# A state-space convolution block on one core: opening redone (x from two queues, output weights folded first, silus over two banks), pair six reordered, the next x's chunks from the third step

## The chip, the cores and the metric

The kernel runs on one core of a Trainium2 chip. Its time is the device time of one execution in microseconds; the time before is the median of three runs, 1819.84 us (1818.55 to 1820.01). The profile is of one further execution, 1821.96 us, of which the profiled span takes 1820.2 us.

## The reference

The input x is (4, 128, 96, 96). It is normalised in 32 groups of channels, read as four sequences of 9216 positions per batch element (rows forward and backward, columns forward and backward), put through the same block four times, and the four results are fused and added to x:

```python
t = _grouped1x1(x, in_proj_w, in_proj_b, G)
u, gate = (t[:, :HID], t[:, HID:])
u = jax.nn.silu(u)
u = lax.conv_general_dilated(u, dw_w, ..., feature_group_count=HID)     # 5 taps
s = _conv1x1(u, ssm_in_w)
a = DMIN + (DMAX - DMIN) * jax.nn.sigmoid(_conv1x1(u, ssm_delta_w, ssm_delta_b))
bb = jnp.tanh(_conv1x1(u, ssm_b_w, ssm_b_b))
cc = jnp.tanh(_conv1x1(u, ssm_c_w, ssm_c_b))
prefix = jnp.cumsum(jnp.log(a), axis=-1)
hst = jnp.exp(prefix) * jnp.cumsum(bb * s * jnp.exp(-prefix), axis=-1)
u = u + _conv1x1(cc * hst + ssm_d[None, :, None] * s, ssm_out_w)
u = _grouped1x1(u * jax.nn.sigmoid(gate), mix_w, mix_b, G)
return _conv1x1(u, out_proj_w, out_proj_b)
...
x = x + fuse(_scan1d of the four sequences of _gn(x))
```

B, DIM = 4, 128; HID, MH, G, K = 256, 32, 4, 5; everything is float32.

## The kernel before

**Tiles and stages.** A batch element is worked in two phases, columns ("V") and rows ("H"), and a phase treats its forward and its backward sequence together, as the units s = 0 and 1. A phase has NS = 6 steps of 16 lines, a step has R = 4 interleaved positions p, so a step is 8 units, worked as 4 pairs. There are 192 pairs in all. In the first half of a phase a step is "fresh": `front` computes the silus of its four position groups g out of x (`in_proj` on PE, `silu` on ACT). In the second half the backward sequence needs what the forward one had, so silus and gates are kept in DRAM (`keep_silu`, `kept`) and loaded again.

**A pair.** `pair(t)` writes the instructions of one pair by hand, for all engines in one order (a manual schedule: each engine and SP's queue run theirs in that order and wait for what they need). It contains:
- the convolution of pair t: half the channels by `taps` (five scaled additions; tap 0 is `first_tap`, on ACT at L628, one pair ahead, the other four are L630 on DVE), the other half by `conv` and `conv_less` on PE, copied to `u` by ACT (L609, L611);
- `front` of the position group four pairs ahead: in_proj (PE, L134 psum<-x_in,wn) and four silus (ACT, L470);
- `proj` (PE, L134 psum<-u,main), then tanh, copy and tanh on ACT (L667, L668, L673) and two operations on POOL (L675, L676); `scale_s` (ACT, L685) scales s of the pair before;
- `scan` on DVE (L702) once per half step, and `outputs` on POOL (L708, L709, L711) five pairs later;
- from pair LAG = 6 on, for the pair bi six pairs back: `gate` (PE, L491), `out_of` (PE, L497), `sigmoids` (ACT, L514), `gating` (DVE, L576 and L577), and one pair later `accumulate`: the output product (PE, L134 psum<-u,w_fin), a copy (ACT, L737) and an addition to acc (POOL, L754).

So pairs 0 to 5 are short, pairs 6 and 7 begin the gating, and from then on all parts run. PSUM has eight banks: 0 to 3 take gating's sums and 0 and 1 of them the taps too; 4 and 5 (PROJ) and 7, 6, 2, 3 (FRONT) change between conv, projection, front and gates. A product that writes a bank waits until ACT or DVE has read what was there.

**The opening.** ACT's queue loads `small`; SP's queue loads x of batch element 0 in ten transfers (24 chunks of 384 positions, 192 KB each) into `acc`, then fuse, main, the first x_in and the gates' x. A transfer is issued only when the one eight before it has landed. DVE takes bn_stats of each chunk (L298). `start()` then writes the rest: some filler products that read acc, `stats_finish` (mean, variance, sqrt, weights times the inverse deviation `wn`, bias `bn`), between its pieces `outer` (out_proj times fuse), then the bursts of in_proj for step 0 and sixteen silus of one bank each, `inner` (mix times that: `w_fin`), the first taps and conv, four keeps of silus, and the bias `b_fin`. x for step 1 is loaded when in_proj of step 0 has read the same tile. `proj` of pair 0 contains step 1's first front.

**The next x.** For batch elements 1 to 3 the statistics are taken during the V phase before: `chunks_of` names two chunks of the next x for the third and fourth pair of each of the six steps; `load_chunks` asks for them two pairs ahead (SP), and DVE takes their bn_stats in the pair (L387).

**What the steps of the prediction touch.** `load_x` (L294 to L298), `stats_finish` (L188 to L256), `chunks_of`, `after_front` and `keep_silu` (L450), `silu` (L470), `sigmoids`, `gates_and_out`, `gating`, `taps`, `proj`, `scale_s` (L685), `pair` and `start` (L992 to L1081).

Of the kernel before, what the change touches and what calls it, by code (L numbers as in the profile page):

```python
# [67 lines left out]
def conv_preact_kernel(  # L68
# [18 lines left out]
    accf = acc.rearrange("p h r m -> p (h r m)")  # L87
    x_in = [big.tile([P, R, N + 1], F32, name=f"x_in{s}") for s in range(2)]
# [65 lines left out]
    gmask = wp.tile([P, 4], F32, name="gmask")  # L154
    nc.gpsimd.memset(gmask, 1.0)
# [13 lines left out]
    stats, free = {}, [FRONT[1]]  # L169
# [10 lines left out]
    def stats_finish(b):  # L180
# [12 lines left out]
        nc.vector.tensor_copy(mean, pm[:, 0:1])  # L193
        dev = sp.tile([P, 1], F32, tag="dev", name=f"dev_{b}")
        nc.vector.tensor_sub(dev, mv[:, 0:1], mean)
        ex = sp.tile([P, 1], F32, tag="ex", name=f"ex_{b}")
        nc.vector.scalar_tensor_tensor(ex, dev, dev, mv[:, 1:2], ALU.mult, ALU.add)
        gm4 = sp.tile([P, 4], F32, tag="gm4", name=f"gm4_{b}")
        nc.vector.tensor_scalar_mul(gm4, gmask, mean)
# [9 lines left out]
        if b == b0:  # L209
# [4 lines left out]
            nc.vector.reciprocal(inv, std)  # L214
        else:
# [11 lines left out]
        yield  # L227
# [11 lines left out]
        product(pb[:, 0:4], wn, gm4)  # L239
        if b == b0:  # L240
            for g in range(4):
                for q in range(R):
                    mm(pb[:, 4 + g : 5 + g], q, wn[0:32, 32 * g : 32 * g + 32], mean[0:32, :], True, True)
            nc.vector.tensor_sub(bn, b_in, pb[:, 0:8])
        else:
# [10 lines left out]
        nc.vector.tensor_scalar_mul(bn[:, 2:4], bn[:, 2:4], 0.5)  # L256
# [8 lines left out]

    def load_front(step, s, r, q):
        if fresh(step):
            un = units[step * UB + s]
            nc.sync.dma_start(
                x_in[s][r, q, :], xs[un["b"], un["lay"], r, q, bass.ds(un["st"] * N, N + 1)]  # L270
            )
# [22 lines left out]
    def load_x(chunks):  # L294
        for c, n in chunks:
            nc.sync.dma_start(accf[:, bass.ds(c * SC, n * SC)], xr[b0, :, bass.ds(c * SC, n * SC)])  # L296
            for e in range(c, c + n):
                nc.vector.bn_stats(stats_of(b0)[:, e, :], accf[:, bass.ts(e, SC)])  # L298
# [5 lines left out]
    nc.gpsimd.memset(first_table, 1.0)  # L304
    nc.scalar.activation(first_table, first_table, AF.Sqrt)
    w_small = load(small, "small", nc.scalar)
    load_x([(0, 1), (1, 1), (2, 1), (3, 2), (5, 2), (7, 3), (10, 4), (14, 4), (18, 4), (22, 2)])
    w_out_fuse = load(fuse, "fuse")
    w_main = load(main, "main")
    for s in range(2):  # L310
        load_front(0, s, half(s), slice(0, R))
    for i in range(UB):
        load_gate(i)
# [50 lines left out]
    gates = [wk.tile([P, 2, 2, N], F32, tag=f"gate{e}", bufs=1, name=f"gate{e}") for e in range(2)]  # L364
# [7 lines left out]
    def chunks_of(t):  # L372

        un = units[2 * t]
        b, k = un["b"] + 1, t % R
        if un["order"] == "V" and b < B and k > 1:
            return [(b, un["st"] * R + 2 * (k - 2) + e) for e in range(2)]
        return []

    def load_chunks(t):  # L380
        for b, c in chunks_of(t):
            chunks[b, c] = wk.tile([P, SC], F32, tag="xs", bufs=4, name=f"xs_{b}_{c}")
# [52 lines left out]
    def after_front(step, g):  # L435
# [7 lines left out]
        if step > 1:  # L443
            keep_silu(1)
# [16 lines left out]
    def in_proj(step, g, s, j, bk):  # L461
        wn = stats[units[step * UB]["b"]][0]
        r = slice(64 * s + 32 * j, 64 * s + 32 * j + 32)
        for c in range(4):
            m, q = (c, g) if j else (g, R - 1 - c if s else c)
            mm(bank(bk), c, wn[r, s, 32 * m : 32 * m + 32], x_in[s][r, q, :], True, True)

    def silu(step, g, s, j, bk):
# [3 lines left out]
            bank(bk)[:, : N + 1],  # L472
            AF.Silu,
# [33 lines left out]
    def sigmoids(bi, to):  # L507
# [3 lines left out]
        for s in range(2):  # L511

            for j in (0, 1) if s == 0 or to[0] == GATE[True][0] else (1, 0):
# [30 lines left out]
    def gates_and_out(bi, with_front):  # L544

        to = GATE[with_front]
# [19 lines left out]
    def gating(bi, s):  # L566
# [8 lines left out]
        if bi not in seeded:  # L575
            nc.vector.tensor_add(pz, pz, v)  # L576
# [13 lines left out]
    def conv(i, banks):  # L590
# [3 lines left out]
        for s in range(2):  # L594
# [21 lines left out]
    def taps(i, ks, first=None):  # L616
# [5 lines left out]
        for k in ks:  # L622
# [6 lines left out]
            else:  # L629
                nc.vector.scalar_tensor_tensor(  # L630
                    us[i][:, :, 1, :] if k == K - 1 else part,
# [9 lines left out]

    def proj(i, banks, apart=False):
# [8 lines left out]
        turns = [(e, j) for j in ((1, 0) if i else (0, 1)) for e in range(2)]  # L651
        apart = apart or not i
        for e, j in sorted(turns) if apart and i else turns:
            if i == 0 and (e, j) == (0, 0):
                first = front_parts(R, (5, 4, 2, 3), half=True)
                next(first)
                next(first)
                first_tap(2)
                for _ in first:
                    pass  # L660
            for c, cols in enumerate(((qb, qb, qa, qa), (qs, qs, qc, qc))[e]):
                first, end = (j == 0, j == 1) if apart else (j == 1, j == 0)
                mm(bank(banks[e]), c, w_proj[:, j, cols], us[i][:, c % 2, j, :], first, end)
# [19 lines left out]
    def scale_s(i):  # L683
        s = tbs[i][0:64, :]
        nc.scalar.activation(s, s, AF.Copy, scale=d_sb[0:64, 0:1])  # L685
# [91 lines left out]
    def pair(t):  # L777
# [13 lines left out]
        if back:  # L791
# [13 lines left out]
        if t:  # L805
            new_u(i)
            taps(i, range(1, K))
            conv(i, banks)
        if t and not ahead:
            conv_less(i, banks)  # L810
        if not back and t:
# [71 lines left out]
        if not old and t > 0:  # L883
            scale_s(i - 2)
        if back:
# [102 lines left out]
    def start():  # L988
        w_of = wp.tile([P, 4, 2, P], F32, name="w_of")

        def filler(n):
            nc.tensor.matmul(  # L992
                bank(7)[:, :n], accf[:, bass.ds(10 * SC, P)], accf[:, bass.ds(10 * SC, n)],
# [3 lines left out]
        def outer(d, i, copy):  # L997
# [5 lines left out]
            copy(w_of[:, d].rearrange("p j c -> p (j c)"), bank(i)[:, : 2 * P])  # L1003

        def inner(ds, i):
# [6 lines left out]
            nc.vector.tensor_scalar_mul(to, bank(i), 0.5)  # L1012
# [160 lines left out]
```

## Time and profile before

| | |
|---|---|
| median of three runs | 1819.84 us (1818.55 to 1820.01) |
| the profiled execution | 1821.96 us, span 1820.2 us |
| busy: PE, ACT, DVE, POOL | 1792.3, 1562.5, 1454.6, 1428.2 us |
| DMA | 321 MB, mean 176 GB/s |
| last bn_stats of the first x ends | 18.82 us |
| first silu | 23.96 us |
| first projection | 35.22 us |
| tanh L667 of pairs 0, 5, 6, 7, 8 | 37.97, 68.50, 78.05, 88.71, 97.89 us |

A line of the timeline gives start and duration in us, engine, source line, operation, what is written and read with its shape, how many were merged, and in brackets the engine's idle time before it and what ended it. A line of the windows gives for each engine its busy time and instruction count, then the granted TensorE clock, the DMA engines' busy share and GB/s. A line of the chain gives start, duration and what the work that ended last waited for or did.

### The profile page before, as it was taken

The numbers are of one execution on the slowest core, as the hardware profiler recorded it, in microseconds if no ns is written. First come the engines' busy times: TensorE is split into PE (matmuls) and PEld (weight loads), VectorE is DVE, ScalarE is ACT, GpSimd is POOL, SyncE is SP. The second block draws the span as 40 slices with busy tenths as digits, with TensorE's granted clock in tenths as the row PEclk, the third lists the DMA queues.
The fourth block names the chain that finished last, engine by engine and source line by source line (L and its number), as shares of the span: only waits on it lengthen the run. The fifth ranks groups of instructions, "written<-read, shape, count | busy, mean of one in ns | idle before, by whom it ended". The sixth has DMA issues, their size and how long they took to land.

```text
span 1820.2 us, 56934 instructions
## 1 busy us (share of the span) xinstructions
PE 1792.3 (98%) x24074; PEld 645.5 (35%) x24074; DVE 1454.6 (80%) x1462; ACT 1562.5 (86%) x2748; POOL 1428.2 (78%) x1475
## 2 busy tenths in 40 slices
PE   6999999999999999999999999999999999999998
PEld 3333333333333333333333333333333333333333
DVE  6888878877888888877778888887877788778885
ACT  4888888988988888888888888888888888888974
POOL 3587878778778888788877888887877888887785
PEclk9999999999999999999999999999999999999999
DMA  8555463444975465334696456453477644635434
GB/s 246 175 190 179 149 203 99 162 142 154 313 242 181 158 196 171 119 135 137 224 296 227 141 179 210 119 171 110 161 237 223 227 148 129 197 102 177 149 125 155
DMA packets 148047, 321.17 MB, mean 176 GB/s; under 512 B 14160, under 2 KB 115920, under 8 KB 147792
## 3 DMA queue, kind: packets, MB, share of 16 engines
q1 hardware_dynamic: 147648, 317.48, 54.2%
q8 instruction: 190, 3.11, 0.7%
q14 instruction: 65, 0.53, 0.1%
q10 hardware_dynamic: 144, 0.04, 0.0%
HBM read 185.21 MB, written 132.25 MB: 174 GB/s over the span
## 4 chain that ended last, share of the span: by engine, by line
PE 94%; ACT 2%; DVE 2%; DMA 1%; issue 0%; SPq 0%; POOL 0%; DVEq 0%; ACTq 0%; POOLq 0%
PE psum L134 81%; PE psum L497 8%; PE psum L491 5%; DMA xs<-in_xr 1%; ACT psum L505 1%; ACT sil L470 1%; DVE psum L630 1%; DMA acc<-in_xr 0%; DVE bn L298 0%; ACT u L611 0%; DVE u L577 0%; DVE u L630 0%; ACT psum L628 0%; DVE t L702 0%; SPq L296 0%
## 5 line engine op out<-in xcount | busy, mean ns | idle before, releaser
L630 DVE SCALAR_TENSOR_TENSOR psum<-sil,small,psum 128x768 f32<-128x768 f32 x576 | 589.0, 1023 | 28.8 <-ACT psum L628 3.4
L134 PE MATMUL psum<-u,w_fin 128*32 128x384 f32 x6176 | 553.1, 488 | 0.2 <-ACT t L673 0.2
L577 DVE SCALAR_TENSOR_TENSOR u<-gate,psum 128x768 f32<-128x768 f32 x376 | 349.8, 952 | 249.0 <-ACT gate L514 107.2
L134 PE MATMUL psum<-u,main 128*32 128x384 f32 x6144 | 534.9, 489 | 1.6 <-DVE u L630 1.5
L754 POOL TENSOR_TENSOR acc<-ys,acc 128x384 f32<-128x384 f32 x374 | 410.7, 1120 | 32.1 <-ACT ys L735 10.8
L708 POOL TENSOR_TENSOR t<-t,t 64x384 f32<-64x384 f32 x191 | 232.3, 1216 | 153.8 <-DVE t L702 70.2
L134 PEld LDWEIGHTS psum<-u,w_fin 128*32 128x32 f32 x6176 | 188.9, 110 | 322.4 <-issue 216.6
L134 PEld LDWEIGHTS psum<-u,main 128*32 128x32 f32 x6144 | 181.9, 109 | 328.4 <-issue 200.7
L505 ACT COPY psum<-u 128x768 f32<-128x768 f32 x352 | 276.7, 799 | 23.1 <-DVE u L630 11.3
L134 PE MATMUL psum<-sil,band 128*32 128x384 f32 x3072 | 285.2, 488 | 0.0
L675 POOL TENSOR_SCALAR t<-tm 64x384 f32<-64x384 f32 x191 | 177.2, 928 | 123.2 <-ACT tm L667 104.2
L709 POOL TENSOR_TENSOR t<-t,t 64x384 f32<-64x384 f32 x191 | 246.8, 1292 | 15.0
L497 PE MATMUL psum<-t,main 32*128 32x384 f32 x1536 | 242.1, 514 | 3.3 <-ACT psum L505 2.6
L628 ACT ACTIVATE psum<-sil,small 128x768 f32<-128x768 f32 x191 | 173.2, 907 | 61.1 <-DVE u L577 52.8
L514 ACT ACTIVATE gate<-psum,bnorm 128x384 f32<-128x384 f32 x384 | 192.1, 582 | 30.1 <-PE psum L491 28.6
L676 POOL TENSOR_TENSOR t<-t,tm 64x384 f32<-64x384 f32 x192 | 195.1, 1016 | 15.3
L630 DVE SCALAR_TENSOR_TENSOR u<-sil,small,psum 128x768 f32<-128x768 f32 x192 | 194.9, 1015 | 7.8
L470 ACT ACTIVATE sil<-psum,bnorm 128x385 f32<-128x385 f32 x384 | 192.1, 585 | 3.7 <-PE psum L134 1.5
L134 PE MATMUL psum<-sil,less 64*32 64x384 f32 x3072 | 168.1, 495 | 0.0
L491 PE MATMUL psum<-x_in,wn 32*128 32x384 f32 x768 | 157.4, 526 | 3.0 <-DVE shift L249 1.4
L711 POOL COPY t<-t 64x384 f32<-64x384 f32 x188 | 141.2, 751 | 15.5 <-PE psum L134 3.6
L134 PEld LDWEIGHTS psum<-sil,band 128*32 128x32 f32 x3072 | 90.3, 109 | 169.6 <-issue 94.4
(102 smaller groups left out, 1484.3 us busy)
## 6 DMA issues: line engine op xcount, KB each, us to landing
sil<-sil SPq DMA_DIRECT2D x128, 770.0 KB, 6.8
kept<-gate SPq DMA_DIRECT2D x80, 768.0 KB, 3.7
gate<-kept SPq DMA_DIRECT2D x76, 768.0 KB, 5.1
x_in<-in_xs SPq DMA_DIRECT2D x192, 96.2 KB, 2.5
out<-acc SPq DMA_DIRECT2D x48, 384.0 KB, 8.0
acc<-in_xr SPq DMA_DIRECT2D x39, 384.0 KB, 6.9
xs<-in_xr SPq DMA_DIRECT2D x72, 192.0 KB, 5.5
x_in<-in_xs SPq DMA_DIRECT2D x46, 192.5 KB, 3.5
```

Of the source, the lines that this page charges most:

```text
L134: nc.tensor.matmul(o[r, : rhs.shape[-1]], lhsT, rhs, start=start, stop=stop, skip_group_check=True)
L470: nc.scalar.activation(sils[step][:, s, j, g, :], bank(bk)[:, : N + 1], AF.Silu, bias=bn[:, 1:2] if j else bn[:, 4 + g : 5 + g],)
L491: nc.tensor.matmul(bank(to)[:, :N], stats[un["b"]][0][r, s, :], x_in[s][r, q, off : off + N], start=True, stop=True)
L497: nc.tensor.matmul(bank(SSM + 2 * s + j)[:, :N], w_so[r, bass.ts(j, P)], z[r, :], start=bi not in seeded, stop=True, skip_group_check=True)
L505: nc.scalar.copy(psum[:, SSM + 2 * s : SSM + 2 * s + 2, :N], us[bi][:, s])
L514: nc.scalar.activation(gv[:, s, j, :], bank(to[2 * s + j])[:, :N], AF.Tanh, bias=bn[:, 2 + j : 3 + j], scale=0.5,)
L577: nc.vector.scalar_tensor_tensor(v, g, 1.0, pz, ALU.add, ALU.mult)
L630: nc.vector.scalar_tensor_tensor(us[i][:, :, 1, :] if k == K - 1 else part, src, w_tap[:, k : k + 1], part, ALU.mult, ALU.add,)
L676: nc.gpsimd.tensor_mul(ta[0:64, p, :], tb[0:64, :], tm[0:64, :])
L708: engine.tensor_mul(ta[0:64, p, :], tb[64:P, :], ta[64:P, p, :])
L709: engine.tensor_add(tb[0:64, :], ta[0:64, p, :], tb[0:64, :])
L754: adder.tensor_add(part, y, part)
```

## The change

It does ten things. (1) x of batch element 0 is asked for from two queues, SP's and ACT's, seven transfers each with small and fuse among them; fuse comes before chunk 10. (2) main is asked for only after bn_stats of chunk 16, through a one-column DVE copy that it has to follow; the gates' x and both steps' x come after it on SP. (3) Step 0 has its own x tile, `x_first`, so step 1's x is loaded in the opening too; the second gate buffer lies in `x_first` later. (4) `outer` and `inner` come before `stats_finish`, with all their copies on ACT; `w_of` uses a slot of the tag "u". (5) In `stats_finish` for the first batch element the bias products use the unscaled weights and a `gm4` that holds the inverse deviation, and the order of a few small operations changes. (6) The sixteen silus of step 0 become eight over two banks each, in an order that starts with a second-half group; five of step 0's taps become two ahead of the others, and DVE does pair 1's first tap. (7) The four keeps of step 0 are issued one per front of step 1, and `b_fin` is computed at the end of pair 2, its addition on DVE. (8) `scale_s` runs on POOL for the first five pairs. (9) In pair 6 the front's silus are split around conv, `out_of` comes before the gates, and both seed additions before both gatings. (10) The next x's chunks are three per pair in the third to sixth steps instead of two in all six.

The diff, cut to its core:

```diff
-    def load_x(chunks):
+    def ask_x(queue, *chunks):
         for c, n in chunks:
-            nc.sync.dma_start(accf[:, bass.ds(c * SC, n * SC)], xr[b0, :, bass.ds(c * SC, n * SC)])
-            for e in range(c, c + n):
-                nc.vector.bn_stats(stats_of(b0)[:, e, :], accf[:, bass.ts(e, SC)])
+            queue.dma_start(accf[:, bass.ds(c * SC, n * SC)], xr[b0, :, bass.ds(c * SC, n * SC)])
+    def stats_x(chunks):
+        for c in chunks:
+            nc.vector.bn_stats(stats_of(b0)[:, c, :], accf[:, bass.ts(c, SC)])
...
+    ask_x(nc.sync, (0, 1), (2, 1), (4, 1), (6, 2))
+    ask_x(nc.scalar, (1, 1), (3, 1))
+    w_small = load(small, "small", nc.scalar)
+    ask_x(nc.scalar, (5, 1), (8, 2))
+    w_out_fuse = load(fuse, "fuse")
+    ask_x(nc.sync, (10, 3), (16, 4))
+    ask_x(nc.scalar, (13, 3), (20, 4))
     nc.scalar.activation(first_table, first_table, AF.Sqrt)
-    w_small = load(small, "small", nc.scalar)
-    load_x([(0, 1), (1, 1), (2, 1), (3, 2), (5, 2), (7, 3), (10, 4), (14, 4), (18, 4), (22, 2)])
-    w_out_fuse = load(fuse, "fuse")
-    w_main = load(main, "main")
+    stats_x(range(17))
+    w_main = wp.tile(list(main.shape), F32, tag="main", name="main")
+    nc.vector.tensor_copy(w_main[:, 0:1], stats_of(b0)[:, 16, 0:1])
+    nc.sync.dma_start(w_main, main)
+    stats_x(range(17, NSC))
     for s in range(2):
         load_front(0, s, half(s), slice(0, R))
+    for s in range(2):
+        load_front(1, s, half(s), slice(0, R))
...
-        if un["order"] == "V" and b < B and k > 1:
-            return [(b, un["st"] * R + 2 * (k - 2) + e) for e in range(2)]
+        if un["order"] == "V" and b < B and k > 1 and un["st"] > 1:
+            return [(b, 3 * (2 * un["st"] + k - 6) + e) for e in range(3)]
...
-        if step > 1:
+        if step > 0:
             keep_silu(1)
...
+    def both_silus(step, g, j, b0):
+        bn = stats[units[step * UB]["b"]][1]
+        nc.scalar.activation(
+            sils[step][:, :, j, g, :],
+            psum[:, b0 : b0 + 2, : N + 1],
+            AF.Silu,
+            bias=bn[:, 1:2] if j else bn[:, 4 + g : 5 + g],
+        )
...
+        to = GATE[with_front] if bi else (4, 5, 7, 6)
+        if bi == 0:
+            for s in range(2):
+                for j in range(2):
+                    out_of(bi, s, j)
+            for s in range(2):
+                for j in range(2):
+                    gate(bi, s, j, to[2 * s + j])
+            sigmoids(bi, to)
+            return
...
-        if bi not in seeded:
+        if bi == 0 and s == 0:
+            for e in range(2):
+                pe = psum[:, SSM + 2 * e : SSM + 2 * e + 2, :N]
+                nc.vector.tensor_add(pe, pe, us[bi][:, e])
+        elif bi and bi not in seeded:
             nc.vector.tensor_add(pz, pz, v)
...
+        if i < 2 * LAG - 2:
+            nc.gpsimd.tensor_scalar_mul(s, s, d_sb[0:64, 0:1])
+            return
...
-        if back:
+        if bi == 0:
+            turned = front_parts(t + R, (2, 3, 7, 6), half=True)
+            next(turned)
+            next(turned)
+        elif back:
             front(t + R, FRONT)
...
+        if bi == 0:
+            for _ in turned:
+                pass
...
+        if t == 2:
+            at_two[0]()
...
+        def b_final():
+            pf = bank(3)[:, 0:1]
+            terms = [(w_of[:, 0, j, :], b_mix[:, j : j + 1]) for j in range(2)]
+            terms.append((w_fuse[:, 0, :], b_out))
+            for c in range(4):
+                for n, (lhsT, rhs) in enumerate(terms):
+                    mm(pf, c, lhsT[:, 32 * c : 32 * c + 32], rhs, n == 0, n == 2)
+            nc.vector.tensor_add(b_fin, pf, b_fuse)
+        at_two.append(b_final)
+        for d in range(4):
+            outer(d, (0, 1, 4, 5)[d])
+        inner((0, 1), 2)
+        inner((2, 3), 3)
...
+        filler(512)
+        filler(256)
+        next(pieces)
+        next(pieces)
+        filler(256)
+        next(pieces)
+        filler(256)
+        next(pieces)
...
+        order = [(1, 0)] + [(0, g) for g in range(R)] + [(1, g) for g in range(1, R)]
+        spots = (D, A, C, D, A, C, A, C)
...
+        for n in range(3):
+            burst(*order[n], spots[n])
+        silus(*order[0], D)
+        burst(*order[3], D)
+        taps(0, (0,), nc.vector)
+        taps(0, (R,), last=3)
+        silus(*order[1], A)
+        burst(*order[4], A)
...
+        silus(*order[7], C)
+        conv_less(0, head_banks(0))
+        taps(0, (3,), last=3)
+        taps(2, (0,), nc.vector)
...
+        front(R, (5, 4, 2, 3))
```

Here D, A and C are the bank pairs (6, 7), (2, 3) and (4, 5).

## The prediction

> **What bounds the kernel now.** First the page: is any engine always busy, and where is it not?
>
> ```profile
> span 1820.2 us, 56934 instructions
> PE 1792.3 (98%) x24074; PEld 645.5 (35%) x24074; DVE 1454.6 (80%) x1462; ACT 1562.5 (86%) x2748; POOL 1428.2 (78%) x1475
> PE   6999999999999999999999999999999999999998
> ```
>
> PE is full in all slices but the first and the last. Listing every start of tanh L667 (one per pair) shows the same: from pair 8 (97.89 us) on the pairs follow each other by 9.11 to 9.33 us, with shorter and longer ones only where a phase or its half changes. So an opening that is redone can only move the moment at which this beat sets in; I forecast that shift. Second, the chain of waits up to 90 us:
>
> ```profile
> 3.62 8.53 DMA acc<-in_xr
> 12.17 6.66 DVE bn L298 x14
> 18.86 0.82 DVE mv L188
> ...
> 36.15 12.76 DMA xs<-in_xr
> 48.94 1.06 DVE bn L387 x2
> ...
> 53.07 1.02 DVE u L630
> 54.23 4.97 PE psum L134 x64
> ```
>
> Until 18.82 the kernel waits for x and its statistics; at 48.94 a chunk of the *next* x ends a wait that pushes taps and projection. Third, the stretches by window: is x held by issue or by transfer?
>
> ```profile
> 2.00:4.00 2.00, 0.00 (x0) 0.00 (x0) 0.37 (x1) 0.74 (x2) 1.81 (x9) 1.00 1.02 254
> 4.00:6.00 2.00, 0.00 (x0) 0.00 (x0) 0.90 (x3) 0.00 (x0) 1.93 (x7) 1.00 0.78 210
> 8.00:12.00 4.00, 0.00 (x0) 0.00 (x0) 3.34 (x7) 0.00 (x0) 2.93 (x8) 1.00 1.03 421
> ```
>
> The last two columns are the DMA engines' share and GB/s: the engines have work from 2 us on, move 210 to 254 GB/s up to 6 us and 421 after. So it is the transfer, not its issue, from 6 us on. Fourth, the timeline, for prices:
>
> ```profile
> 24.90 5.32 ACT L470 ACTIVATE sil<-psum,bnorm 128x385 f32<-128x385 f32 x11 [0.36 <-PE psum L134]
> 48.00 1.99 ACT L470 ACTIVATE sil<-psum,bnorm 128x385 f32<-128x385 f32 x4
> 48.94 1.06 DVE L387 BATCH_NORM_STATS2 bn<-xs 128x6 f32<-128x384 f32 x2 [2.38 <-DMA xs<-in_xr]
> 55.35 1.42 SPq L450 DMA_DIRECT2D sil<-sil  x1
> 79.16 0.88 PE L134 MATMUL psum<-x_in,wn 32*32 32x385 f32 x16 [0.57 <-DVE u L577]
> 186.19 1.82 DVE L577 SCALAR_TENSOR_TENSOR u<-gate,psum 128x768 f32<-128x768 f32 x2 [1.08 <-PE psum L497]
> ```
>
> The first row is eleven silus back to back (0.484 each), the second the four silus behind projection 2, then the late chunk, one keep of silus (770 KB, its issue held), PE waiting for pair 6's gating, and DVE's idle time in a steady pair with chunks.
>
> **The change, in five stretches.** Marks of before: last bn_stats ends 18.82; first silu 23.96; projections of pairs 0 to 7 (PE, psum<-u,main) start at 35.22, 41.48, 47.32, 54.23, 60.08, 65.83, 75.00, 86.53.
>
> *1. x (to the last bn_stats).* ACT's issues (0.41 each) cost nothing: ACT idles until 20.73. Each queue now gets seven transfers before the last bn_stats, and fuse (512 KB) moves ahead of chunks 10 to 23. Landings before: chunks 0 to 4 by 7.87, 0 to 23 by 16.92, so 19 chunks (3648 KB) in 9.05 us, 403 KB/us. After: 3648+512 KB at that rate is 10.3 us. If the ramp is as before, x is in at 7.87+10.3 = 18.2; if both queues reach the plateau from the first bytes (2.2), at 2.2+(960+4160)/403 = 14.9. No row shows two large queues at once, so I take the middle, 16.6. The queues are paired size for size, so the last two transfers (16-19 and 20-23) should land together, and eight bn_stats of 0.475 plus the 0.2 us marker copy for main still follow: end at 20.6 (18.9 to 22.2). Before, DVE had only 1.9 us left after the last landing. **+1.8** (+0.1 to +3.4). [...] Main is held until bn_stats 16, and x_first, step 1's x and all gate loads queue behind it on SP: main (384 KB, 1 to 1.85 us) and two halves of x_first (1.75 each, 20.35 to 22.10 to 23.86 before) arrive some 2.5 to 3.4 us after the last bn_stats, before they are needed; if later, all is late by that.
>
> *2. Last bn_stats to first silu.* Before 5.14, as the second half of x_in landed only at 23.86. After: the 3.74 us to wn lose the mean copy (0.19) and the wait behind outer (some 0.2), gain gm4 (0.24): 3.6; then in_proj 0.33 issue and 0.5 latency: 4.45. Outer and inner ran after the last bn_stats; now they follow fuse (in by about 10) with their copies on ACT, and with the fillers are over between 17 and 19, so PE idles 3 to 5 us before the mean product (1.0 before). Two readings show what that may do: the filler's matmuls are 0.85 us apart up to 16.5 and 0.43 after, and in the tail a half-idle stretch is followed by half the granted clock (the column after POOL):
>
> ```profile
> 1794.00:1798.00 4.00, 1.98 (x12) 0.89 (x10) 2.57 (x4) 1.98 (x3) 3.74 (x4) 1.00 0.02 4
> 1798.00:1804.60 6.60, 6.60 (x37) 1.89 (x36) 1.91 (x2) 2.66 (x5) 5.35 (x5) 0.51 0.19 74
> ```
>
> I charge 0.4 for a first burst at half speed (0 to 1.5): 4.85. **-0.3.**
>
> *3. First silu to projection 0.* Before 11.26: sixteen silus of 0.484 with inner's 2 us and b_final between. After: eight silus over two banks, 0.80 each (L611, the same width out of PSUM, 0.799), end 6.85 after the first, one slot lost to PE; the last tap adds 1.02 and handoffs end at 8.05; conv_less and u's copy (0.80) end at 8.15 beside it. Projection 0 at 8.2. POOL's w_of adds (3.3 us, once main has come) and edges, and DVE's first two taps, hide under the silus; if they did not, the adds would delay the edges by about their own length. The front of step 1 (four silus, 2.0) fits between u's copy and projection 0's tanh. **-3.06** (0.5 either way).
>
> *4. Pairs 0 to 5, projection to projection.* Before 6.26+5.84+6.91+5.85+5.75 = 30.61. Undisturbed, PE's order (projection 2.28, conv 1.75, less 0.81, in_proj 1.03) makes 5.87. The chunk stall goes: pair 3 alone had 6.91. scale_s on POOL (0.93, POOL is idle 3.7 to 4.9 us per pair) frees 0.62 of ACT that PE's beat hides. But two waits come. b_final now stands behind projection 2 on PE and needs bank 3, which the last silu of that front frees 2.7 us after the projection's start (48.00+1.99 against 47.32 above); conv 3 waits behind it, and its tensor_add on DVE ends at 3.6, with pair 3's four taps (4.15, and 0.1 to PE) queued behind: projection 3 at 7.85, **+2.0** on 5.87 (at least +1.0, since without bank 3's wait it follows the projection itself). And the keeps of step 0, four in a row at 32 to 36 us before, now go out one per front, the last in pair 3, while pair 4's first silu reuses that tile. The row at 55.35 is the same place in SP's queue, behind the four x loads of pair 3: it landed at 61.98, and the silus stood at 60.76. Some 1.2 us of wait on ACT; behind it stand that pair's tanh and the banks of conv 5, so 0.83 on PE (0 to 2). Sum 5.87+5.87+7.87+5.87+6.70 = 32.18. **+1.6.** (-0.2 to +2.8)
>
> *5. Pairs 6 and 7.* out_of comes before the gates, so DVE's seed adds start some 2 us earlier; gating ends at 11.05 after projection 5 instead of 13.27, and the 0.57 of idle at 79.16 goes, as does pair 7's bn_stats. PE's next conv_less moves from 15.57 to 14.2 and all behind it with it: **-1.25** (-1.4 to -0.5). Later pairs: a third bn_stats (0.5) meets at least 1.08 us of DVE idle (186.19): 0. If that cover were gone, 24 pairs by up to 0.5.
>
> Sum: 1.8-0.3-3.06+1.6-1.25 = -1.2 on the profiled execution (1821.96, span 1820.2), which stands 2.1 above the median; on the median 1819.84 that is **1818.6**. What stage 3 gains, stages 1 and 4 give back.
>
> **Rivals.** *A, faster:* both queues run at the plateau at once, bn_stats end at 18.9, PE stays at full clock (-0.4), the keep lands in time (-0.8), b_final costs only 1.0. -1.2-1.7-0.4-0.8-1.0 = -5.1, 1814.7. For it: the slow stretch up to 6 us is that of the single chunks, with the shortest rows (1536 bytes), which a second queue could overlap; against: the engines' share is 1.02 from 2 to 4 us already.
>
> *B, slower:* TensorE stays at half clock through projection 0 and pair 1. Stage 3 would gain conv 0.65, less 0.65, front 0.65, projection 2.3 = 4.25 behind the last silu, pair 1 again 4.9: -1.6+9.1 = +7.5, 1827.3. It decides from about 1 us after projection 0's end. For it: the tail's row of 0.51 after a half-idle stretch; against: burst and conv at half speed keep PE 80% busy. [...]
>
> *C, the second queue does nothing:* ramp as before, end at 22.2, +0.4 in all, 1820.2.
>
> **How the numbers follow.** 0.2% (3.6 us) is about what a measurement here can tell from no change. My forecast 0.32 and C 0.20 lie within it: same 0.52. A and its neighbours below 1816.2: faster 0.33. B and a later x: slower 0.15. The low bound is A's time less 1.0, half of what it would bring if chunks 16-19 landed one transfer (1.9) ahead of 20-23; the high one is the slow ends of stages 1, 2 and 4 together (1.6+1.1+1.2 above the forecast, 1822.5) and 1 us of B.
>
> **What would show it.** Right: last bn_stats near 20.6, with eight after one landing; projection 0 near 33.6; a DVE wait for b_final's matmuls after pair 2 and an ACT wait on a keep in pair 4; pair 5 where it was; pair 7 1.25 earlier; then 9.11. Wrong: x in by 15.5, projection 0 before 32 or after 36, granted clock 0.5 beyond 34, or pairs after 8 off their beat.

## The result, and the profile after

The changed kernel takes 1829.73 us (median of 6 runs, 1828.0 to 1830.32) beside 1819.92 for the kernel before (6 runs): ratio 1.005 [1.004, 1.0059], slower by half a per cent. The forecast was 1818.6, with 1823.5 as the high end. The profiled execution took 1830.32 (span 1828.6), 8.4 more than that of before, and the tanh of pair 8 (now L713) starts at 106.43 instead of 97.89, 8.54 later; the beat behind it is 9.11 as before. So the loss lies wholly in the first 100 us, and the marks split it:

| stretch | before | after | change | forecast |
|---|---|---|---|---|
| 1. to the end of the last bn_stats | 18.82 | 23.50 | +4.69 | +1.8 |
| 2. to the first silu | 5.14 | 6.21 | +1.06 | -0.3 |
| 3. to projection 0 | 11.26 | 13.09 | +1.83 | -3.06 |
| 4. projection 0 to 5 | 30.61 | 33.20 | +2.59 | +1.6 |
| 5. projection 5 to 7 | 20.70 | 19.06 | -1.64 | -1.25 |

Executions of one kernel differ, and the longest have the lowest mean granted clock (before: 31 executions taken together, from 1818.57 to 1827.74, clock 0.999 to 0.994); each ratio below is therefore against the kernel before on the same chip at the same time, over all executions (it is not the ratio of the two medians), and mechanisms are read from the marks. A mark comes from one trace of each kernel.

First the page of the changed kernel. The first slice, of 45.7 us, is the only one that differs much from before: PE 5 tenths (6 before), granted clock 0.7.

```profile
span 1828.6 us, 56961 instructions
PE   5999999999999999999999999999999999999998
PEclk7999999999999999999999999999999999999999
```

Second, its chain of waits (start, length, what):

```profile
6.36 13.28 DMA acc<-in_xr
19.66 1.94 DVE bn L311 x4
21.60 0.05 DVE main L328
21.65 1.86 DVE bn L311 x4
...
57.97 0.16 DVE b_fin L1083
...
63.21 5.89 DMA sil<-sil
...
71.66 0.13 ACT sil L499
```

x comes to 19.63 (16.92 before), and eight bn_stats stand behind the last landing, as forecast. The marker copy for main (L328) runs after twenty bn_stats and not after seventeen: the program was not run in its written order. SP's issues say the same, with x_first (two halves of step 0's x) 12.9 us ahead of main:

```profile
8.79 1.31 SPq L280 DMA_DIRECT2D x_first<-in_xs  x2
21.68 0.34 SPq L329 DMA_DIRECT2D main<-in_main  x1
```

Further down the chain stand the two waits that were forecast, b_final's add and a keep ahead of pair 4's silus. Third, the windows (the column after POOL is the granted clock, then the DMA engines' share and GB/s):

```profile
20.00:24.00 4.00, 0.00 (x0) 0.00 (x0) 3.96 (x10) 0.00 (x0) 0.00 (x0) 0.62 0.35 86
24.00:28.00 4.00, 3.52 (x72) 2.17 (x76) 1.78 (x9) 1.48 (x2) 0.38 (x1) 0.50 1.07 243
28.00:32.00 4.00, 4.00 (x79) 1.86 (x78) 1.41 (x4) 2.50 (x5) 0.18 (x2) 0.50 0.74 177
36.00:40.00 4.00, 4.00 (x40) 0.63 (x32) 1.69 (x2) 1.62 (x2) 0.00 (x0) 0.50 0.01 4
```

TensorE has nothing at all from 20 to 24, and from then on half the clock: the trace's clock records have 0.5 from 20.96 to 41.44. In the last two rows PE is full (4.00 of 4) while the number of matmuls in a window falls to 40, and ACT, which should bound the silus, is busy 1.62 of 4. Fourth, rows of the timeline (start, busy, what, and the idle time before it with its releaser):

```profile
24.48 0.29 PE L135 MATMUL psum<-mv,gmean 128*32 128x1 f32 x8 [7.17 <-DVE mv L190]
57.97 0.16 DVE L1083 TENSOR_TENSOR b_fin<-psum,small 128x1 f32<-128x1 f32 x1 [4.18 <-PE psum L135]
62.37 2.79 PE L135 MATMUL psum<-u,main 128*32 128x384 f32 x32 [1.44 <-DVE u L681]
71.66 2.00 ACT L499 ACTIVATE sil<-psum,bnorm 128x385 f32<-128x385 f32 x4 [2.57 <-PE psum L135]
72.77 1.50 PE L135 MATMUL psum<-sil,band 128*32 128x384 f32 x16 [1.76 <-ACT sil L499]
```

The 7.17 us of idle time ahead of the mean product had been forecast as 3 to 5. DVE's 4.18 ahead of b_fin and PE's 1.44 ahead of projection 3 are b_final's wait; ACT's 2.57 and PE's 1.76 are the keep's. ACT's row names PE because the profile puts a wait for several things down to one; the chain names the keep, whose landing it puts at 69.10, and leaves 2.48 us behind it unexplained. The two runs below that change only the order and the queues of the opening's loads have the same wait (2.55 and 2.37 on ACT) and a full record of the landing: the silus start at 69.72 and 68.12, 0.15 behind the landing of that keep (69.57 and 67.97). So the keep most likely landed at about 71.5 here.

### The profile page after: what moved, and what is told of

Read it like the earlier page. It is cut to its first block, busy times and chain, and to the rows that moved or that the text cites. A ratio compares the mean times of both kernels' runs of the same rounds, so it can differ in the third digit from the quotient of the medians.

```text
span 1828.6 us, 56961 instructions
## 1 busy us (share of the span) xinstructions
PE 1794.7 (98%) x24088; PEld 646.7 (35%) x24088; DVE 1451.7 (79%) x1453; ACT 1558.1 (85%) x2736; POOL 1438.0 (79%) x1489
## 4 chain that ended last, share of the span: by engine, by line
PE 95%; ACT 2%; DMA 1%; DVE 1%; issue 0%; ACTq 0%; DVEq 0%; SPq 0%
PE psum L135 82%; PE psum L535 8%; PE psum L529 5%; DMA acc<-in_xr 1%; ACT psum L543 1%; ACT sil L499 1%; DVE psum L681 0%; DMA sil<-sil 0%; ACT u L662 0%; DMA small<-in_small 0%; DVE bn L311 0%; ACT psum L679 0%; PE psum L1054 0%; DVE u L681 0%; DVE u L628 0%
## 5 line engine op out<-in xcount | busy, mean ns | idle before, releaser
L628 DVE SCALAR_TENSOR_TENSOR u<-x_first,psum 128x768 f32<-128x768 f32 x188 | 174.9, 953 | 127.3 <-ACT x_first L552 61.0
L628 DVE SCALAR_TENSOR_TENSOR u<-gate,psum 128x768 f32<-128x768 f32 x188 | 174.8, 953 | 115.5 <-ACT u L660 57.1
L499 ACT ACTIVATE sil<-psum,bnorm 128x385 f32<-128x385 f32 x368 | 183.9, 583 | 4.7 <-PE psum L135 2.6
```

The source lines that it names most:

```text
L499: nc.scalar.activation(sils[step][:, s, j, g, :], bank(bk)[:, : N + 1], AF.Silu, bias=bn[:, 1:2] if j else bn[:, 4 + g : 5 + g],)
L628: nc.vector.scalar_tensor_tensor(v, g, 1.0, pz, ALU.add, ALU.mult)
```

## The experiments

**Is it the gap on TensorE, through the clock?** The changed kernel with six more fillers of 512 columns:

```
-        filler(512)
-        filler(256)
+        for n in (512,) * 7 + (256,):
+            filler(n)
```

> Six more filler matmuls of 512 columns on TensorE ahead of the mean product, where the changed kernel has 7.17 us of idle time. Theory (idle TensorE brought the half clock, and the half clock made the opening long): granted clock 1.0 from about 14 us on; last bn_stats unchanged at 23.5; first silu about 5.4 after it (6.20 with the half clock); projection 0 starts 8.5 after the first silu (13.09), so about 37.4 instead of 42.80; all later marks 5.4 earlier; median about 1824.4. Rival 1 (the eight silus and their handoffs set the length, the clock little): clock 1.0, but projection 0 still 11 or more after the first silu, gain under 2.5, 1827.3 or more. Rival 2 (the clock falls for another reason than idle time): 0.5 from about 21 us again, 1829.7.

Measured: 1824.57 (ratio to before 1.0024 [1.0014, 1.0033]). Windows:

```profile
20.00:24.00 4.00, 2.81 (x8) 1.14 (x6) 3.97 (x10) 0.00 (x0) 0.00 (x0) 1.00 0.44 111
24.00:28.00 4.00, 2.99 (x100) 1.92 (x101) 1.95 (x10) 1.69 (x3) 0.39 (x1) 1.00 1.08 240
28.00:32.00 4.00, 3.67 (x90) 1.02 (x63) 2.10 (x3) 3.61 (x5) 0.56 (x6) 1.00 0.74 175
```

The last bn_stats ends where it did (23.51), the clock stays at 1.0, the first silu comes 4.89 behind it (4.85 forecast) and projection 0 9.38 behind that, at 37.77. Compared with the changed kernel's 6.21+13.09 the half clock costs 5.03 of stretches 2 and 3. In four other traces with the half clock (the runs below on order, queue, b_final and keeps) the two stretches take 19.2 to 20.3, against 14.27 here. Where stretch 3 still misses the forecast (9.38 against 8.2), ACT waits for PE's products: idle 0.43 and 0.73 ahead of the last two silus and 0.69 ahead of u's copy. The ten executions range from 1822.05 (clock 0.997) to 1829.01 (0.993): some still meet the half clock, and the traced one, at 0.998, does not show where.

**Does idle time do the same to the kernel before?** Its six fillers taken out:

```
-        for n in (512, 512, 512):
-            filler(n)
-        for n in (512, 512):
-            filler(n)
-        filler(128)
```

> The kernel before, without its six filler matmuls: TensorE has nothing to do until the mean product at 19.8. Theory (idle TensorE alone brings the half clock, whatever the opening's order): granted clock 0.5 when the chain begins and until about 35 to 41, last bn_stats unchanged at 18.8, first silu 0.5 to 1.2 later, projection 0 3 to 5 us later than 35.22; tanh of pair 8 at 101 to 103; median 1823 to 1825. Rival (the half clock in the changed kernel comes from its small in_proj matmuls and the fillers matter little): clock 1.0 within 4 us of the first products, projection 0 under 1.5 later, median under 1821.5.

Measured: 1826.49, ratio 1.0024 [1.0009, 1.0038]; last bn_stats at 18.26, first silu 7.75 behind it (5.14), projection 0 at 40.53 instead of 35.22. The trace has no clock record before 34.60, where 1.0 begins; the durations tell:

```profile
24.44 6.99 PE L134 MATMUL psum<-x_in,wn 32*32 32x385 f32 x96
31.36 3.58 PE L1007 MATMUL psum<-w_of,fuse 128*128 128x128 f32 x16
```

The same rows in the kernel before:

```profile
23.07 4.58 PE L134 MATMUL psum<-x_in,wn 32*32 32x385 f32 x96
27.58 2.05 PE L1007 MATMUL psum<-w_of,fuse 128*128 128x128 f32 x16
```

TensorE was slow through all its bursts, and full speed was there at the end of the 3.41 us that inner's 128-row matmuls fill to 95%. `outer`, which has 128 rows too, had filled 78% of an earlier such stretch (20.95 to 24.37) and not brought it back. With TensorE idle ahead of the chain (for 7.17 us in the changed kernel, until 19.25 here) either opening was slow, which speaks for the theory; in this trace the loss was larger than expected. But the gap is not enough by itself: of the ten executions six take 1825.9 to 1828.3 and four 1820.2 to 1823.0, near the kernel before.

**Why did it stay down for 20 us of busy work?** Three wide fillers in the middle of the changed kernel's bursts, at half clock:

```
             burst(*order[n], spots[n])
+        for _ in range(3):
+            filler(512, 0)
         silus(*order[0], D)
```

> The changed kernel, with three filler matmuls of 128 rows by 512 columns behind the first three bursts of in_proj, that is, in the middle of the stretch at half clock. [...] Rival (once lowered the clock stays down for a set time, three periods of 6.83 us): back at 41.4 as before, projection 0 some 4 to 5 us later; median over 1833.

```profile
28.00:32.00 4.00, 4.00 (x35) 1.58 (x19) 0.06 (x1) 2.49 (x3) 0.37 (x4) 0.50 0.45 110
32.00:36.00 4.00, 4.00 (x45) 1.51 (x50) 0.95 (x1) 0.07 (x1) 0.00 (x0) 0.66 0.00 0
36.00:40.00 4.00, 3.06 (x71) 0.55 (x44) 2.48 (x5) 3.32 (x4) 0.59 (x5) 1.00 0.01 4
```

The clock is back at 34.68, and not at 41.4 as in the rival; 5.3 us of fillers lengthen the way from the last bn_stats to projection 0 by only 1.1 (20.4 against 19.3); 1828.18, ratio 1.0023 [1.0013, 1.0033]. The clock's records change in steps of 3.41 us, called periods here. Both kernels had PE 100% busy in a full period before (27.79 to 31.20 in the changed one, with bursts and, up to 28.18, small products; 27.85 to 31.27 here, 45% of it fillers) and stayed at half clock; the clock came back behind the period that the fillers filled (31.27 to 34.68). Busy time as the profile shows it thus did not tell, in these two traces, whether the clock came back.

**x: order and queues.** First the same loads and bn_stats kept in the order in which they are written:

```
+    with tc.manual_schedule(engines={nc.vector.engine, nc.sync.engine, nc.scalar.engine}):
         ask_x(nc.sync, (0, 1), (2, 1), (4, 1), (6, 2))
         ...
         for i in range(UB):
             load_gate(i)
```

> The loads of x, its bn_stats, main and x_first are kept in the written order on SP, ACT and DVE: chunks 10-12 before 13-15, 16-19 before 20-23, main behind bn_stats 16, x_first behind main. Theory (DVE waited for chunks in another order than they landed, and x_first took bandwidth from the last chunk): last chunk lands at about 18.0 instead of 19.63, last bn_stats ends at about 21.5 instead of 23.51; all later marks 2.0 earlier if the clock falls as before; median about 1827.7. Rival 1 (x_first takes nothing): last chunk still at 19.6, end at 21.6 by the order alone. Rival 2 (the order costs nothing, since the last four bn_stats stand behind the last landing either way): gain under 0.5, 1829.3.

Chain of waits:

```profile
6.71 10.15 DMA acc<-in_xr
16.86 0.02 issue
16.89 0.57 DVE bn L311
17.46 0.02 issue
17.48 0.15 DVE main L329
17.64 3.23 DVE bn L311 x7
```

The last chunk lands at 17.08 instead of 19.63, and the last bn_stats ends at 20.86 instead of 23.50; 1827.11, ratio 1.0038 [1.0023, 1.0052]. In the changed kernel the two halves of x_first were issued at 8.79 and 9.50, ahead of main, and shared the engines (share 1.03 from 8 to 16 us, 0.95 from 16 to 20) with the last chunk: the first half landed at 20.35; and DVE took chunks 13-15 (landed 15.36) ahead of 10-12 (13.21), and 20-23 (19.63) ahead of 16-19 (17.55). Held in order, both go, and the last chunk comes earlier than the 18.0 expected: the rival in which x_first takes nothing (19.6) is out. Five traces with the changed kernel's own loads end their bn_stats between 22.26 and 23.51, so the gain is 1.4 to 2.6. The half clock stays (20.47 to 40.95).

Then, in this order, all of x from SP's queue:

```
-        ask_x(nc.sync, (0, 1), (2, 1), (4, 1), (6, 2))
-        ask_x(nc.scalar, (1, 1), (3, 1))
+        ask_x(nc.sync, (0, 1), (1, 1), (2, 1), (3, 1), (4, 1), (5, 1), (6, 2), (8, 2))
...
-        ask_x(nc.sync, (10, 3), (16, 4))
-        ask_x(nc.scalar, (13, 3), (20, 4))
+        ask_x(nc.sync, (10, 3), (13, 3), (16, 4), (20, 4))
```

> As the run in written order, but all of x is asked for on SP's queue, in the order of its columns; only small is on ACT's. Theory (two queues share the engines and end together; one queue delivers in order, so fewer bn_stats are left behind the last landing): last chunk lands at about 18.2, last bn_stats ends at 20.2 (four behind the last landing), 1.3 earlier than with two queues in the written order. Rival (the second queue shortens the start, where single chunks of 1536-byte rows move slowly): last chunk lands at 18.8 to 19.5, last bn_stats ends at 20.8 or later, no better than two queues.

The last chunk lands at 18.12, 1.04 later than from two queues, yet the last bn_stats ends at 20.24, 0.62 earlier (1826.01, ratio 1.003 [1.0018, 1.0042]). From two queues chunks 16-19 and 20-23 land together, at 16.86 and 17.08; from one, 16-19 is in at 16.24 and four bn_stats run while 20-23 is still on its way. What counts here is when the first four of the last eight chunks are in. The expected end of 20.2 held, the difference of 1.3 was too large. These are single traces: four kernels below with the same loads from one queue have the last chunk at 17.54 to 17.80 and end at 19.67 to 19.93, so one queue gains 0.6 to 1.2 over the one trace with two. Two queues brought the last byte 1.04 us earlier than one did in this trace and 0.5 to 0.7 earlier than in those four (159 against 131 GB/s in the first 4 us and 324 against 305 in the next four, this trace); the end of the statistics did not gain at all.

**b_final alone** back at the end of the opening:

```
-        if t == 2:
-            at_two[0]()
...
         for _ in pieces:
             pass
+        b_final()
```

> Only b_final (twelve small matmuls and one add on DVE) goes back from behind projection 2 to the end of the opening. Theory (the add waits for the bank that the last silu of the front frees, and pair 3's taps wait behind the add): projection 2 to projection 3 falls from 7.97 to 5.9; projection 0 comes up to 0.5 later; tanh of pair 8 about 1.7 earlier; median about 1828.0. Rival (the 2 us were cover for another wait, such as the keep that stands before pair 4's silus): the interval falls, but projections 4 to 5 or 5 to 7 give it back, and the tanh of pair 8 stays within 0.4 of 106.4.

Projection 2 to 3 falls from 7.97 to 5.75, but 3 to 4 grows from 5.84 to 7.42:

```profile
65.93 0.21 PEld L135 LDWEIGHTS psum<-x_in,wn 32*32 32x32 f32 x16 [1.66 <-ACT u L662]
66.69 0.18 PEld L135 LDWEIGHTS psum<-x_in,wn 32*32 32x32 f32 x16 [0.54 <-DMA x_in<-in_xs]
```

Step 2's x, loaded where step 1's front is done, is now late: two of its loads land at 65.83 and 66.65, and PE's work on them begins 0.10 and 0.04 later (the first row names ACT's copy of u, but in the changed kernel the same products start before that copy does, at 67.19 and 67.37). Projection 4 to 5, where the keep is awaited, falls to 7.02. The three intervals together are 1.4 shorter than their 21.6; 1828.72, ratio 1.0048 [1.0033, 1.0063]. The rival was partly right: b_final's two us had covered an x load.

**The keeps alone** back at the opening's end:

```
-        if step > 0:
+        if step > 1:
             keep_silu(1)
...
+        keep_silu(R)
         front(R, (5, 4, 2, 3))
```

> Only the four keeps of step 0 go back to the end of the opening, issued together, and the keeps of later steps begin one step later. Theory (in pair 4 the silus wait for a keep of step 0, held behind pair 3's four x loads and sharing the DMA engines with step 1's keeps): projection 4 to projection 5 falls from 7.78 to 5.9, ACT's idle time of 2.57 before pair 4's silus goes; tanh of pair 8 1.7 earlier than 106.43; median about 1828.0. Rival 1 (the keeps only change place and now hold up the x loads of step 1 or 2, as in the run without b_final's wait, where the x load of step 2 took 1.57 back): the interval falls, but another of projections 0 to 4 grows by over 1 us and the gain is under 0.6. Rival 2 (the wait is for bandwidth and not for the order): 7.78 stays within 0.4.

Projection 4 to 5 is 5.76 (7.78), 3 to 4 is 5.91; 1828.25, ratio 1.004 [1.0031, 1.005]. Pair 4's silus start 0.75 behind projection 4 (67.53), with no wait:

```profile
68.28 1.98 ACT L499 ACTIVATE sil<-psum,bnorm 128x385 f32<-128x385 f32 x4
```

So the wait is the keeps', worth 2.0 here, and the other intervals did not pay for it. With the keeps unmoved projection 4 to 5 varied: 6.09 with more fillers, 6.24 with fillers in the middle, 7.02 with b_final moved, 7.58 from one queue, 7.77 in written order, 7.78 in the changed kernel.

**The parts behind the opening, in the kernel before.** Chunks alone (`st > 1`, three per pair, six buffers; `ident` lies in `w_fin` to make room):

> The kernel before with one part of the change alone: three chunks of the next x per pair from the third step on, none in pairs 2 and 3 (a small tile shares another's place to make room). Theory: the wait for the late chunk ahead of projection 3 goes, 6.91 falls to 5.9; pair 7 has no bn_stats; later pairs with a third bn_stats keep their 9.11 beat; tanh of pair 8 1.0 earlier than 97.89; median 1818.8. Rival (what stood behind the chunk takes its place, as x loads or keeps do in the changed kernel): 6.91 falls by under 0.3, median within 0.4 of before. Second rival (the third bn_stats shows in 24 later pairs): beat over 9.15 there, median over 1822.

Projection 2 to 3 falls to 5.75 as expected, and 3 to 4 rises from 5.84 to 6.34, so 0.66 is left of 1.16; the beat stays 9.11. Nor is this 0.66 clear of the differences between traces: projection 2 to 4 takes 12.09 here and 12.75 in the kernel before, but 12.39 and 13.06 in two other runs with the chunks unmoved (pair six alone, no fillers). Time: 1820.53, ratio 1.0003 [0.9991, 1.0015], which does not resolve it either; its profiled execution also had the half clock from 25.45 to 32.28, so its projection 0 (38.46) says nothing of the chunks.

Pair six alone (the branch for `bi == 0` in gates and outputs, both seed adds at once, `turned`):

> The kernel before with pair six's new order alone (outputs ahead of gates, both seed adds at once, step 2's last front in two parts). Theory: projections 0 to 5 stay, projection 5 to 7 falls from 20.70 to 19.3 (19.06 in the changed kernel, which also has no bn_stats there); tanh of pair 8 1.3 earlier; median 1818.5. Rival (the saving is given back by the wait for x or gates in pair 7, which before began later): the sum of the two intervals falls by under 0.4.

Projection 5 to 7 takes 18.99 (20.70), a gain of 1.71; 1818.5, ratio 0.9986 [0.9976, 0.9997]: faster.

Both, and scale_s on POOL, behind the opening of before:

> The kernel before with its own opening, and with what the change does behind it: chunks three per pair from the third step, pair six's order, scale_s on POOL in the pairs ahead of the ninth. Theory (the parts behind the opening gain, the opening loses): projection 2 to 3 and 3 to 4 together 0.7 less, projection 5 to 7 about 1.7 less; tanh of pair 8 2.4 earlier than 97.89; median 1817.5, ahead of both kernels. Rival (they cover each other): no better than pair six alone, 1818.5.

From the first silu to the tanh of pair 8: 71.79 (73.93 before), 2.1 less; projection 5 to 7 in 19.11, 2 to 4 in 12.35 (12.75). 1820.04 beside 1822.56 of the kernel before on that chip: ratio 0.9985 [0.9974, 0.9995]. This version beats both kernels; beyond pair six alone the gain is not resolved.

**Can the new opening be mended?** One queue in written order, three more fillers ahead and a longer one in the chain, the keeps at the opening's end:

> The changed kernel with what the runs found mended: x from one queue in the written order, three more fillers ahead of the mean product and a longer one in the chain, the keeps of step 0 at the opening's end; b_final stays behind projection 2. Theory: last bn_stats at 20.2, clock 1.0 from 15 on, first silu at 25.1, projection 0 at 34.4, projection 2 to 3 still 7.97, 4 to 5 at 5.8; tanh of pair 8 at about 96.3, 1.6 ahead of before; median 1818.5. Rival (the mends do not add up, and the shorter opening meets the x loads of step 1 and 2): over 1821.

The same with b_final at the opening's end:

> As the mended kernel, and b_final back at the end of the opening. Theory: projection 2 to 3 falls from 7.97 to 5.8 and, with the keeps out of the way of the x loads of step 2, projection 3 to 4 stays under 6.5; tanh of pair 8 about 1.5 to 2 ahead of the mended kernel; median 1816.8. Rival (the x loads of step 2 bind as in the run with b_final alone moved, 7.42): gain under 0.6, 1818.

Neither: 1824.62, ratio 1.0008 [0.9999, 1.0017], and 1825.16, ratio 1.0011 [1.0, 1.0023]. Statistics and first silu came as expected (19.67 and 24.73 in the first), but the clock fell again, from 29.15 to 39.39 in the one and from 32.34 to 42.58 in the other, with no gap ahead of the bursts; projection 0 at 39.08 and 39.20. In both the last period before the fall has PE waiting 0.71 for ACT; it also stops for 0.80 and 0.42 in the middle of a burst, in the first kernel behind the fall, in the second ahead of it. With b_final moved, projection 2 to 3 falls to 5.75 as expected, and 3 to 4 takes 6.92 (under 6.5 expected, 7.42 the rival); projection 0 to 1 takes 7.40 instead of 5.88, its first 3.4 us at half clock. So two wide fillers went inside:

```
         silus(*order[0], D)
+        filler(128, 0)
         burst(*order[3], D)
...
         silus(*order[4], A)
+        filler(384, 7)
         burst(*order[6], A)
```

> The mended kernel (one queue, written order, more fillers ahead, keeps at the opening's end), whose clock fell in the middle of its bursts (0.5 from 29.15 to 39.39 in its profile, after a window in which bursts of 32 by 32 filled 79%), with two fillers of 128 rows inside the opening, 128 columns ahead of the fourth burst and 384 in the 0.71 us of wait ahead of the seventh. Theory (thin bursts with a gap do not hold the clock; a little wide work does): clock 1.0 from 16 to the tail, projection 0 at 9.0 to 9.6 after the first silu (14.35 without), so 33.7 to 34.3; tanh of pair 8 at about 96; its fast executions 4 to 5 us below the mended kernel's and within 1.5 of, or below, before's. [...]

> As the run before it in this call, with b_final at the opening's end instead of behind projection 2. Theory: projection 2 to 3 5.75 instead of 7.98, projection 0 to 1 up to 0.6 longer for the twelve small products, projection 3 to 4 up to 6.9 as the x loads of step 2 then bind (0.60 of wait for them in the mended kernel with b_final moved): tanh of pair 8 0.5 to 1.5 earlier than with b_final behind projection 2, 94.5 to 95.5, that is 2.4 to 3.4 ahead of before; its full-clock executions near 1817. Rival (the x loads take all of it back): no difference between the two.

1824.26, ratio 1.0002 [0.9992, 1.0012], and 1822.19, ratio 0.9998 [0.9989, 1.0007]. In the first of the two:

```profile
28.00:32.00 4.00, 3.07 (x38) 0.76 (x26) 1.40 (x3) 2.00 (x4) 0.60 (x5) 1.00 0.99 299
32.00:36.00 4.00, 4.00 (x40) 0.59 (x40) 1.51 (x2) 1.65 (x2) 0.00 (x0) 0.50 1.08 254
```

```profile
30.95 0.84 PE L135 MATMUL psum<-x_first,wn 32*32 32x385 f32 x5 [0.93 <-issue]
31.84 0.90 ACT L506 ACTIVATE sil<-psum,bnorm 128x770 f32<-128x770 f32 x1 [2.00 <-PE psum L135]
```

The fall comes later (32.01) and lasts 6.8 us instead of 10.2, and 3.4 in the second; projection 0 at 38.87 and 38.13. The fillers closed the wait for ACT, but PE stops for 0.93 in the middle of a burst, with no releaser in the profile, and the clock falls behind that. That the stop brings the fall is not shown: PE is busy for 73% and 74% of the period ahead of it, and the run with fillers in the middle kept its clock through a period of 72% (34.68 to 38.09). What stops PE is open too: a 16 KB packet of an instruction queue took 1.2 us shortly before, on DMA engines with a share of 0.99, and the stop came after the 15th of the burst's 16 matmuls in both mended kernels and, with four more matmuls ahead, after the 11th. The run with six more fillers has such a packet at 30.16, 1.2 us long as well, and no such stop; none of this was followed up. b_final at the opening's end is worth 2.23 in projection 2 to 3 (7.98, 5.75) at 0.41 in 3 to 4 (5.84, 6.25), with projection 0 to 1 unchanged. From the first silu to projection 0 the two take 13.90 and 13.04, against 9.38 at full clock. The half clock accounts for part of this alone: 6.8 and 3.4 us at half speed can cost at most 3.4 and 1.7 of these 4.5 and 3.7 us. Whether a mended opening could beat the versions built on the opening of before was not shown.

## Why the prediction was wrong

*Stretch 1, +4.69 for +1.8.* The size of the transfer was right: with the written order x is in at 17.08 and the last bn_stats end at 20.86, beside 16.6 and 20.6 forecast. The 16.6 was the middle between two bounds, so that it was met is in part luck. What failed is the sentence that x_first, step 1's x and the gate loads queue behind main on SP, and with it the assumption that DVE takes chunks as written. The part of the program ahead of the hand-ordered section is ordered by the planner, the tool that orders the instructions where the program does not; before, with one queue, its order and the landings agreed, and I took that for a rule.

*Stretches 2 and 3, +2.9 for -3.36.* The step that failed is the 0.4 (0 to 1.5) charged for the clock. I had counted 3 to 5 us of idle TensorE (7.17, of which 2.9 come from stretch 1), had the tail's row of 0.51 before me, and let the clock recover behind the first bursts because they keep PE busy. That a first burst at half speed would be all was my estimate, and no run shows it: a period that the bursts fill (27.79 to 31.20, PE busy for all of its 3.41 us) was followed by 0.5 again, and the clock stayed down for 20.48 us. Measured, the half clock costs 5.03, 4.6 more than the 0.4 charged. The other 1.6 of the miss are there at full clock as well: the handoffs between bursts and double silus, forecast as 8.2 and measured as 9.38, and 0.4 in stretch 2 (4.89 against 4.45 without the charge). The 6.85 for the eight silus does not follow from its own prices either: eight of 0.80 are 6.4, and with a slot lost 7.2. Rival B, 1827.3, had the half clock but not its place: it put it through projection 0 and pair 1 and charged 9.1, while the clock was back at 41.44, before projection 0 (42.80). That its time comes near 1829.73 is chance, since the rest comes from x, the handoffs and the keep. I gave it and a later x 0.15 together, since "burst and conv at half speed keep PE 80% busy" counted busy time, and a period with PE 100% busy (27.79 to 31.20) did not bring the clock back.

*Stretch 4, +2.59 for +1.6.* b_final's interval was forecast as 7.87 and is 7.97, with the wait on the row named. The keep was the right wait in the right place, but 1.9 and not 0.83 on PE: the term was sized from one keep's landing in pair 3 of before (6.6 us from issue). In the changed kernel it is about 8.3 (by the start of the silus), and 8.3 and 8.1 in the two runs with the same wait; in three other runs with the same three keeps behind it, it landed 6.1 to 6.3 us from issue, and projection 4 to 5 is 0.2 to 0.4 over the undisturbed 5.87 in two of them. So the size that was forecast lies between those of different runs, and the keeps that follow do not explain the difference by themselves; what does is open. The run with the keeps moved shows only that the wait is theirs.

*Stretch 5, -1.64 for -1.25.* Right in sign and nearly in size; the kernel before with pair six alone gains 1.71. Right as well: the beat from pair 8 on, the wait for the chunk gone, the third bn_stats hidden.

The sum missed by 9.7: 2.9, 6.3 and 1.0, less 0.4. Rivals A and C fell on the same clock; A's hope of an end at 18.9 was not reached by any of the orders run.

## What to carry to other kernels

When work moves out of a stretch that waits for data, look at what the engine left behind does there: this opening, which folds weights early, left TensorE idle for 7.17 us later, and the half clock that followed taxed the next 20.5 us. Before a transfer's place in a queue enters a sum, find out whether that part of the program runs as written. A removed wait is worth what is left when the next late thing arrives: of b_final's 2.2 us, 0.6 remained in one kernel and 1.8 in another.

## What the runs showed of the hardware

In these traces the granted clock changes on a grid of 3.41 us (records of 3.41, 6.83, 10.2, 13.65, 20.48). In the changed kernel a period with no matmul (17.55 to 20.96) was followed by 0.5. For other periods the traces show this (without fillers, where the record begins at 34.60, the clock is read from durations: 6.99 us for 96 products of in_proj, 4.58 in the kernel before):

- Not followed by the full clock, although PE was busy for 97 to 100% of them: bursts of 32 rows by 32 columns, with small products only in the first 0.4 us (27.79 to 31.20 in the changed kernel, and 24.37 to 31.19, two periods, in the kernel before without fillers), and products of 128 rows by 128 columns in 71% and 78% of a period (24.37 to 27.79 in the changed kernel, 20.95 to 24.37 without fillers).
- Followed by the full clock: periods that products of 128 rows by 128 columns fill to 81%, 95% or 100% (28.86 to 32.28 with the chunks moved, 31.19 to 34.60 without fillers, 31.27 to 34.68 with fillers in the middle), and in the changed kernel one with none of them, filled by in_proj, conv and conv_less (38.03 to 41.44).
- At full clock, PE's busy share did not tell where it fell: periods of 67 to 79% were followed by the fall in the mended kernels, and one of 90% in the kernel before with the chunks moved (22.04 to 25.45); periods of 51% and 79% in the run with more fillers (21.54 to 24.95, 31.78 to 35.19) and of 72% with fillers in the middle (34.68 to 38.09) were not, nor was one of 97%, bursts alone, in the kernel before (23.20 to 26.61).

What sets the clock these runs do not say.
